# Layer 0 of a four-layer convolution network on one core: rows of x and residual rows are issued from GpSimd's queue instead of SP's

## The chip, the core and the metric

The program runs on one core of one Trainium2 chip. The metric is the device time of one execution in microseconds (us); lower is better. Three runs of the kernel before gave 6715.55, 6727.29 and 6740.69 us, with a median of 6727.29 us. Engines are named as in the profile: PE is TensorE's matmul and PEld its weight load, DVE is VectorE, ACT is ScalarE, POOL is GpSimd and SP is SyncE. A "q" behind a name (SPq, POOLq) is that engine's own sequence of waits and DMA issues.

## The reference, cut to what matters

The input x has the shape (4, 64, 256, 256) in float32. Four layers follow one another, each of the form x + f(group_norm(x)). Only layer 0 is touched by the change:

```
x = x + _L0_conv_ref(_gn(x), w_in, w_dw, fft_filter, w_out)

def _L0_conv_ref(x, w_in, w_dw, fft_filter, w_out):
    x = einsum('bchw,oc->bohw', x, w_in)            # 64 -> 384 channels
    xf = rfft2(x in 8x8 patches) * fft_filter ; x = irfft2(xf)
    x = conv2d(x, w_dw, padding=1, groups=384)      # depthwise 3x3
    x1, x2 = split(x, 2, axis=1)
    return einsum('bchw,oc->bohw', gelu(x1) * x2, w_out)   # 192 -> 64
```

Layers 1 to 3 are a 3x3 convolution, a gated "center or periphery" convolution, and a truncated Fourier layer.

## The kernel before, in words

**Tiling of layer 0.** A picture has 32 rows of 8x8 patches. One row of patches of one picture is a tile `x` of 128 partitions (64 channels times two halves of the width) by 8 lines of 128 values. `load_x` (line 414) loads it with two DMAs of 256 KB, one for each half of the width (line 418); on the side of the memory each line is a run of 128 floats, 512 bytes. `normalize_x` (L256) turns the tile into `xn` on ACT. `p_x` has four such tiles, which are shared with the tiles `st`, from which the statistics of the next picture are taken (lines 614 to 618, runs of 4 KB).

**Blocks.** The work goes in 12 blocks `p`, three for each picture, of up to 12 rows of patches. In a block, four channel groups `kb` follow one another. Each has an *expand phase* of 11 or 12 calls of `expand` (PE at line 443 multiplies `xn` with `win`; ACT and DVE copy the result to `u`, lines 450 to 452) and then 12 calls of `convolve` (g = 0 to 11; PE at lines 483 and 492; Gelu on ACT at line 499, product on DVE at line 500, result `h`). Each `h` is stored to a scratch tensor `g` in the memory by POOL (line 503); four `h` tiles take turns (`p_h`), so the Gelu of step g+4 needs the store of step g to have landed.

**The block before is projected meanwhile.** After g = 1, 4, 7 and 10, `project` does one half of one line r (0 to 7) of the block before: SP loads the needed planes of `g` (`load_g`, lines 535 and 539), `load_r` (line 548) loads the residual lines `r` of x with two DMAs of 320 or 352 KB, again in runs of 512 bytes, PE multiplies (lines 580 and 587), DVE adds into `r` (lines 596, 599, 601) and takes statistics (L607), and after the second half POOL stores `r` (line 611, two DMAs in runs of 512 bytes). Two `r` tiles take turns, so `load_r` of line r+2 must wait for the stores of line r to have landed. The weights `w` are loaded by SP (line 460). After the last block, the projection of it runs alone (the *tail*), with three `r` tiles.

**What sets the order.** A block of the program (`tc.manual_schedule`) keeps PE, DVE, ACT and SP in the order in which the program is written. POOL isn't in that list: the framework's planner sets the order of POOL's instructions, and with it the place of each DMA that POOL issues. The framework also puts in the waits: the DMAs of one kind of queue use eight semaphores in turn, so a DMA waits for the one issued eight places ahead of it, besides waiting for its tile to be free.

Of the kernel before, what the change touches and what calls it, by code (L numbers as in the profile page):

```python
# [121 lines left out]
class _Net:  # L122
# [152 lines left out]
    def _layer0(self, ctx, dst):  # L275
        tc, nc, a, B, H, W = self.tc, self.nc, self.a, self.B, self.H, self.W
# [9 lines left out]
        P = PATCH  # L286
        HW2 = W // 2
# [10 lines left out]
        halves = [slice(0, C), slice(C, 128)]  # L298
# [9 lines left out]
        p_xn, p_x = pool("l0xn", NR + 1), pool("l0x", 4)  # L308
# [20 lines left out]
        p_s = ctx_a.enter_context(tc.tile_pool(name="l0as", bufs=7))  # L329
# [73 lines left out]
        xns, x0, wl, st, gs, bst0s, bst1, loads, rts = ({} for _ in range(9))  # L403
# [7 lines left out]
            (blocks[p][0], blocks[p][1] + t) for t in range(NR + 1) if 0 <= blocks[p][1] + t < NP  # L411
        ]

        def load_x(row, p_x=p_x):
            b, i = row
            x0[row] = p_x.tile([128, P, HW2], F32, tag="x", name=f"x0_{b}_{i}")
            for s in range(2):
                nc.sync.dma_start(x0[row][halves[s]], a["x"][b, :, P * i : P * i + P, s * HW2 : (s + 1) * HW2])

        def normalize_x(row):  # L420
            b, i = row
# [94 lines left out]
        def rows_in(p, r):  # L516

            b, i0 = blocks[p]
            lo, hi = (max(0, -i0), NR) if r < P - 1 else (0, min(NR, NP - 1 - i0))
            return lo, hi, i0 + lo + (r == P - 1), (r + 1) % P  # L520
# [23 lines left out]
        def load_r(p, r):  # L544
            lo, hi, j0, rr = rows_in(p, r)
            rt = rts[p, r] = sources[p == NB - 1][2].tile([128, NR, HW2], F32, tag="r", name=f"r_{p}_{r}")[:, 0 : hi - lo]
            for s in range(2):
                nc.sync.dma_start(
                    rt[halves[s]], xr(a["x"][blocks[p][0]])[rr][:, j0 : j0 + hi - lo, s * HW2 : (s + 1) * HW2]
                )  # L550

        def load_half(p, r, half):
            if 0 <= p < NB and r < P:
                if half == 0:
                    load_r(p, r)
                load_g(p, r, half)
# [73 lines left out]
        with ordered:  # L630
# [24 lines left out]
                first_stats(k + 7)  # L655
            rows = rows_of(0)
            for row in rows[:7]:
                load_x(row, p_s)
            for row in rows[7:11]:
                load_x(row)  # L660
            for j in range(3):
                load_w(j)
            self.group_norm(0, 0, bst0, avgs)
# [18 lines left out]
            for p in range(NB + 1):  # L682
# [22 lines left out]
                b, i0 = blocks[p]  # L705
# [8 lines left out]
                for kb in range(4):  # L714
                    for t in range(NR + 1):
                        if 0 <= i0 + t < NP:
                            expand(p, kb, t)
                    for g in range(NG):
                        G = NG * kb + g
                        if g % 2 == 0:  # L720
                            load_w(p * (HID // 8) + G // 2 + 3)
                        convolve(p, kb, g)
                        if g < NG - 1:
                            self.next_norms()
                        if g in (1, 4, 7, 10):
                            unit()
                        if kb < 3:
                            if g % 3 == 0:
                                if len(loaded) == 2 or not nk:
                                    for k in loaded[: 1 if nk else 2]:  # L730
                                        next_stats(b + 1, loaded.pop(0))
                                if nk:
                                    k = nk.pop(0)
                                    load_stats(b + 1, k)
                                    loaded.append(k)
                            if kb == 2 and g == NG - 1:
                                for row in fresh[:4]:
                                    load_x(row)
                        elif 0 <= g - 1 < len(fresh):
                            k = g - 1  # L740
                            normalize_x(fresh[k])
                            if k + 4 < len(fresh):
                                load_x(fresh[k + 4])
# [731 lines left out]
```

## Time and profile before

| what | value |
|---|---|
| median of 3 runs (lowest, highest) | 6727.29 us (6715.55, 6740.69) |
| the profiled execution's own time | 6742.27 us |
| its span, first to last instruction | 6740.5 us |
| layer 0 | about 0 to 4165 us of the span |
| of it: tables, statistics, first rows | about 0 to 118 us |
| of it: tail (last block's projection alone) | about 4040 to 4163 us |
| PE busy in 340 to 4030 us | 3263.54 of 3690 us |
| DMA engines busy in 340 to 4030 us | 0.75 of 16 engines, 208 GB/s |
| POOL busy in 340 to 4030 us | 536.62 us |

The time of layer 0 follows from the page's lines of it: the first and the last store of `r` (line 611) start at 452.8 and 4165.5 us. In the page, part 3 gives the DMA queues. q1 is the queue that SP issues to, q10 the one of ACT, q0 the one of POOL, and q8 brings the engines their instructions. "Packets" are the units in which a queue's DMAs are worked off, and the share is the time that they took of the 16 DMA engines' span. In lists of waits, `PE psu L443 <- issue` means that PE stood idle ahead of a matmul of line 443 and that no other engine's work was what it waited for. The times of matmuls are modelled[...].

### The profile page before, as it was taken

What the parts mean: (1) busy time and instruction counts of PE and PEld (TensorE: products, weight loads), DVE (VectorE), ACT (ScalarE), POOL (GpSimd) and SP (SyncE); (2) the same over time, 40 slices, a digit from 0 to 9 for tenths busy, and PEclk for the clock granted to TensorE, in tenths of its full rate; (3) what the DMA queues carried; (4) which work ended last, traced back from release to release, by engine and by line L of the source; (5) the groups of instructions that cost most, each with busy time, mean ns of one, the idle gap of its engine ahead of it and who ended that gap; (6) DMA issues with size and microseconds to landing.
All of it is one profiled execution on the core that took longest, in us unless ns stands there. A gap on an engine that the chain in (4) does not pass through costs nothing.

```text
span 6740.5 us, 255130 instructions
## 1 busy us (share of the span) xinstructions
PE 5980.4 (89%) x115416; PEld 3144.4 (47%) x115416; DVE 4125.0 (61%) x5652; ACT 3098.0 (46%) x4292; POOL 1050.2 (16%) x1646
## 2 busy tenths in 40 slices
PE   3988888888888888888999885999899999999988
PEld 1445444445444545444455443333344444443476
DVE  5545454555454555454554454999788888885355
ACT  4343433343333343334333331777787777774211
POOL 3111111111111111111111110111022222221011
PEclk9999999999999999999999996999999999999855
DMA  8577778777777777777777759999766666667889
GB/s 238 154 192 207 213 210 216 206 213 207 212 210 216 207 213 207 215 210 208 206 208 206 204 175 239 241 228 228 178 169 172 177 168 177 168 176 251 322 348 400
DMA packets 878574, 1448.75 MB, mean 215 GB/s; under 512 B 77252, under 2 KB 586452, under 8 KB 875444
## 3 DMA queue, kind: packets, MB, share of 16 engines
q1 hardware_dynamic: 725284, 923.09, 54.0%
q0 software_dynamic: 148672, 500.14, 21.2%
q8 instruction: 911, 14.93, 1.0%
q10 hardware_dynamic: 3536, 9.20, 0.6%
q14 instruction: 171, 1.40, 0.1%
HBM read 932.08 MB, written 500.04 MB: 212 GB/s over the span
## 4 chain that ended last, share of the span: by engine, by line
PE 78%; issue 7%; DMA 6%; ACT 4%; DVE 4%; SPq 0%; POOL 0%; ACTq 0%; DVEq 0%; POOLq 0%
PE pc L492 17%; PE pc L483 12%; PE psu L443 11%; PE m L858 10%; PE one L1099 8%; PE div L1058 6%; PE po L580 4%; DMA x<-x 2%; PE po L587 2%; PE psz L1088 2%; DMA g<-g 2%; PE psa L1286 2%; PE psy L1433 1%; ACT u L450 1%; ACT u L452 1%
## 5 line engine op out<-in xcount | busy, mean ns | idle before, releaser
L443 PE MATMUL psu<-win,xn 64*64 64x96 f32 x34816 | 1003.8, 266 | 399.8 <-issue 323.9
L500 DVE TENSOR_TENSOR h<-h,pc 128x374 f32<-128x374 f32 x1152 | 574.7, 541 | 1269.6 <-ACT h L499 1268.5
L499 ACT ACTIVATE h<-pc 128x374 f32<-128x374 f32 x1152 | 492.8, 480 | 1827.8 <-PE pc L492 1815.9
L492 PE MATMUL pc<-u,w 64*16 64x374 f32 (+2 forms) x27648 | 1247.8, 484 | 0.2 <-issue 0.2
L443 PEld LDWEIGHTS psu<-win,xn 64*64 64x64 f32 x34816 | 908.0, 148 | 516.5 <-issue 384.1
L483 PE MATMUL pc<-u,w 64*64 64x374 f32 x9216 | 912.6, 493 | 70.6 <-DVE u L452 69.1
L503 POOL DMA_DIRECT2D g<-h x576 | 416.7, 723 | 3211.9 <-DVE h L500 2998.7
L492 PEld LDWEIGHTS pc<-u,w 64*16 64x16 f32 (+2 forms) x27648 | 414.6, 92 | 769.6 <-issue 767.9
L1044 DVE TENSOR_TENSOR q<-xn 128x2313 f32<-128x2313 f32 (+2 forms) x256 | 627.9, 2495 | 1.9 <-ACT xn L256 1.7
L1099 PE MATMUL one<-z,wp 32*32 32x512 f32 x16384 | 599.0, 598 | 19.8 <-issue 16.4
L450 DVE COPY u<-psu 128x384 f32<-128x384 f32 x544 | 303.7, 558 | 490.2 <-PE psu L443 462.9
L256 ACT ACTIVATE xn<-x,nb,r 128x1024 f32<-128x1024 f32 (+3 forms) x272 | 486.8, 1793 | 242.6 <-DMA x<-x 142.0
L483 PEld LDWEIGHTS pc<-u,w 64*64 64x64 f32 x9216 | 340.0, 133 | 516.6 <-issue 353.6
L1045 ACT ACTIVATE q<-q 128x2313 f32<-128x2313 f32 (+2 forms) x256 | 529.0, 2086 | 29.6 <-DVE q L1044 28.7
L450 ACT COPY u<-psu 128x384 f32<-128x384 f32 x544 | 288.3, 530 | 530.2 <-PE psu L443 522.9
L1058 PE MATMUL div<-q,ones 64*32 64x512 f32 x8192 | 471.2, 600 | 14.6 <-ACT q L1045 9.4
L1099 PEld LDWEIGHTS one<-z,wp 32*32 32x32 f32 x16384 | 367.1, 103 | 233.6 <-issue 93.1
L1132 POOL DMA_DIRECT2D x<-r x512 | 275.4, 547 | 977.8 <-DVE r L1129 953.7
L580 PE MATMUL po<-g,wo 128*64 128x176 f32 (+1 forms) x3072 | 315.0, 348 | 62.1 <-DMA g<-g 39.2
L858 PE MATMUL m<-t,wk 64*64 64x512 f32 x3072 | 341.1, 588 | 0.0
L580 PEld LDWEIGHTS po<-g,wo 128*64 128x64 f32 x3072 | 210.3, 141 | 212.9 <-issue 114.9
L452 DVE COPY u<-psu 64x384 f32<-64x384 f32 x544 | 304.9, 560 | 7.4
(158 smaller groups left out, 6440.0 us busy)
## 6 DMA issues: line engine op xcount, KB each, us to landing
g<-h POOLq DMA_DIRECT2D x576, 374.0 KB, 7.1
x<-x SPq DMA_DIRECT2D x240, 640.0 KB, 6.5
w<-wt SPq DMA_DIRECT2D x288, 448.0 KB, 7.9
x<-x SPq DMA_DIRECT2D x100, 1024.0 KB, 14.1
g<-g SPq DMA_DIRECT2D x414, 187.0 KB, 5.5
g<-g SPq DMA_DIRECT2D x736, 93.5 KB, 6.1
x<-in_x_dram SPq DMA_DIRECT2D x256, 256.0 KB, 8.2
x<-o POOLq DMA_DIRECT2D x128, 512.0 KB, 8.2
```

What stands on the lines that cost most here:

```text
L443: nc.tensor.matmul(ps[s][halves[1 - odd], k, at], xn[halves[s], n + odd].rearrange("p r w -> p (r w)"), win[halves[s], kb, PB * (1 - odd) ...
L450: copy(at(slice(0, 128), 8 * s + 1), v[:, 0:PB])
L483: nc.tensor.matmul(out(C * c, C, k, h), w[halves[h], k, 2 * (G % 2) + c, 0:C], cells(h, 4 * g + 2 * k + c, 0, 0), start=True, stop=False, ...
L492: nc.tensor.matmul(out(q, m, k, h), w[halves[h], k, 2 * (G % 2) + c, c0 : c0 + m], cells(h, 4 * g + 2 * k + c, down, right), start=False, ...
L499: nc.scalar.activation(h[:, k], ps[k][:, 0, 0:L], AF.Gelu)
L500: nc.vector.tensor_mul(h[:, k], h[:, k], ps[k][:, 1, 0:L])
L580: nc.tensor.matmul(out(k, s, x), wo1, moving(g1[:, 2 * k], 2 * half + k, s, x), start=(x == 0), stop=False, skip_group_check=True,)
L858: nc.tensor.matmul(rows2(m)[halves[j], s], w[dx][halves[s]], ts[n][halves[s], i, 2 * j : 2 * j + 2, dx : dx + W], start=(dx == 0), stop=(d ...
L1044: nc.vector.tensor_sub(d, p0, p1)
L1045: nc.scalar.activation(d, d, AF.Square)
L1058: ins = nc.tensor.matmul(ps[quarters[j], h], ones[halves[h]], q[n, g, k][halves[h], r + 2 * j : r + 2 * j + 2, o : o + W], start=(m == 0), ...
L1099: ins = nc.tensor.matmul(rows2(ps[g])[quarters[j], k], w[quarters[i]], z[quarters[i], h, 2 * j + dy : 2 * j + dy + 2, dx : dx + W], tile_p ...
```

## The change

`load_x` gets an argument `queue`, which is POOL's by default, and `load_r` issues from POOL. The first 11 rows of the program (22 DMAs) still come from SP. So 117 of 128 rows of x (234 DMAs of 256 KB) and all 96 residual tiles (192 DMAs of 320 or 352 KB), 426 DMAs, are issued by POOL. What is transferred, and in which runs, stays the same.

```
-        def load_x(row, p_x=p_x):
+        def load_x(row, p_x=p_x, queue=nc.gpsimd):
...
             for s in range(2):
-                nc.sync.dma_start(x0[row][halves[s]], a["x"][b, :, P * i : P * i + P, s * HW2 : (s + 1) * HW2])
+                queue.dma_start(x0[row][halves[s]], a["x"][b, :, P * i : P * i + P, s * HW2 : (s + 1) * HW2])
...
             for s in range(2):
-                nc.sync.dma_start(
+                nc.gpsimd.dma_start(
                     rt[halves[s]], xr(a["x"][blocks[p][0]])[rr][:, j0 : j0 + hi - lo, s * HW2 : (s + 1) * HW2]
                 )
...
             for row in rows[:7]:
-                load_x(row, p_s)
+                load_x(row, p_s, nc.sync)
             for row in rows[7:11]:
-                load_x(row)
+                load_x(row, queue=nc.sync)
```

On PE, DVE and ACT the order of the instructions is the same in both programs. On SP the 426 DMAs are gone from between the loads of `g`, `w` and `st`. On POOL the planner put them between the stores. Here is the compiled order of POOL's queue in block 1 (counted from 0), channel group 3, around g = 4 (the number behind h is g, and what stands in brackets is what the DMA waits for besides the semaphore of the DMA eight places ahead):

```
L503 store h 4
L418 load x, fresh row 7, first half   [ACT: its tile was normalized]
L611 store r line 6, both halves       [DVE: line 6 was added]
L418 load x, fresh row 7, second half
L548 load r line 0 of block 1, first half   [the two stores of r line 6, just above, have landed]
L503 store h 5                         [DVE]
L418 load x, fresh row 8, both halves  [ACT]
L548 load r line 0, second half
L503 store h 6                         [DVE]
L418 load x, fresh row 9, both halves  [ACT]
L503 store h 7                         [DVE]
```

In channel groups 0 to 2 the same stands there without the rows of x: store h 4, store r (both halves), load r (first half, waits for the two stores), store h 5, load r (second half), store h 6. The same pair of r store and r load stands between h 10 and h 11. The first four rows of x of a block are placed in channel group 2, between the stores of h 5 and h 10.

## The prediction

> **What bounds the kernel now.** I read the page's parts 1 to 3, then what PE waited for in the steady part of layer 0 (340 to 4030 us), then the windows, queues and order of time of single stretches.
>
> ```profile
> PE 5980.4 (89%) x115416; PEld 3144.4 (47%) x115416; DVE 4125.0 (61%) x5652; ACT 3098.0 (46%) x4292; POOL 1050.2 (16%) x1646
> ...
> q1 hardware_dynamic: 725284, 923.09, 54.0%
> q0 software_dynamic: 148672, 500.14, 21.2%
> q8 instruction: 911, 14.93, 1.0%
> ```
>
> PE is the bound; POOL has room. A packet on q0 is 3.4 KB (500.14 MB / 148672) although the residual stores in it are runs of 512 bytes, so this queue joins runs. One on q1 is 1.3 KB. q8 brings instructions in pieces of 16 KB.
>
> ```profile
> PE psu L443 <- issue: 312.7, 177, 5.9
> PE pc L483 <- DVE u L452: 65.2, 53, 2.5
> PE psu L443 <- ACT u L452: 37.7, 112, 1.2
> ```
>
> In layer 0's steady part PE waits for no data load at all. Its largest wait, 312.7 us, is "issue", and nearly all of it is in the expand phases. There are 44 full ones there, so 7.1 us in each. The next view (window, PE, PEld, DVE, ACT, POOL, clock, DMA share, GB/s) says when:
>
> ```profile
> 3802.00:3814.00 12.00, 8.80 (x296) 7.98 (x292) 6.95 (x14) 6.41 (x13) 1.06 (x2) 0.86 0.92 267
> 3815.00:3827.00 12.00, 9.60 (x383) 8.63 (x380) 9.31 (x17) 8.69 (x17) 0.00 (x0) 1.00 0.02 4
> 655.00:667.00 12.00, 8.64 (x272) 7.98 (x270) 6.83 (x13) 6.30 (x13) 0.00 (x0) 0.78 1.04 201
> ```
>
> The first two rows are halves of one expand phase. With the DMA engines busy PE gets through 296 matmuls in 12 us, with them idle 383. The third row has the DMA engines full of rows of x and residual rows: 272 matmuls, and only 201 GB/s. Its queue:
>
> ```profile
> q1 hardware_dynamic: 4111, 2.37, 102.1%
> ```
>
> That is 1.021 x 16 x 12 us / 4111 = 48 ns for each packet of about 512 bytes. So the runs of 512 bytes fill the DMA engines at a poor rate, and while these are full PE's instructions come late.
>
> In the tail (4040 to 4160 us) the DMA engines are the bound outright:
>
> ```profile
> q1 hardware_dynamic: 15073, 15.17, 57.2%
> q10 hardware_dynamic: 3536, 9.20, 31.2%
> q0 software_dynamic: 1789, 5.76, 14.7%
> ```
>
> Here a q0 packet of 3.2 KB, nearly all from stores in runs of 512 bytes, takes 0.147 x 16 x 120 / 1789 = 158 ns. That is 25 ns for 512 bytes, against 48.
>
> **What the Trainium skill says.** (1) "DMA: Bandwidth & Descriptors", section "SWDGE vs HWDGE vs iDMA": GpSimd's DMAs have their descriptors made by software, and a packet preferably holds up to 4096 bytes. The 3.4 KB agree for stores; no load on q0 is in this trace. (2) Same page, "Issuing engines are not separate DMA queues": all queues share the 16 engines, and another issuer saves only issue time. If that were all, nothing would be won here; the 48 against 25 ns speak against "only". (3) "Runtime: NRT & Kernel Launch", "Instruction fetch mechanics": instructions come in blocks of 16 KiB through a DMA queue of the engine's own, "mostly hidden". q8's piece agrees, the 312.7 us say that here it isn't hidden. (4) First page, "Anatomy of one DMA": a semaphore wait is held by the issuing sequencer. So a wait for a tile now holds up POOL's stores; no trace here shows it yet.
>
> **Part by part.** The sum is made against the profiled execution's own 6742.3 us (span 6740.5), 15.0 us above the median of the runs.
>
> *Rows of x.* Summed for each expand phase in order of time, the "issue" waits average 9.0 us in channel group 0 and 8.4 in group 3, 5.7 and 5.6 in groups 1 and 2. Rows of x are loaded just there: in group 3's expand phase, and in its steps up to group 0's. The excess is 3.0 us in 22 phases, 67 us. After, the first four rows are issued some 10 us earlier, and a row of 4 KB per partition should be one packet instead of eight. I take two thirds, **-45 us**; ends 0 and -67.
>
> *Residual rows.* Half of the 88 pairs fall to the expand phases, one each: 2 x 704 packets x 48 ns / 16 = 4.2 us of full DMA engines, after at 25 ns 2.2 us. An expand phase loses 7.1 us in some 20 us of busy DMA engines, 0.35 us for each; 2.0 x 0.35 x 44 = 31 us. I take **-26**, since residual loads now start nearer to the phase's start; ends 0 and -31.
>
> *Tail.* 16 residual DMAs of about 700 runs, 11,200 x (48 - 25) ns / 16 = 16 us of a stretch that is full of DMA. The loads of `g` also wait for one another there; **-12**; ends 0 and -16.
>
> *SP relieved.* SP held these issues up to 9.3 us, and its loads of `g` and `w` come sooner. PE waits for neither outside the tail, so 0.
>
> *POOL's own time.* A load isn't in the POOL trace; the nearest row is the residual store, 0.78 us for 640 to 704 runs. 426 x 0.78 = 332 us on an engine that is busy 537 of 3690. Cost 0, save two issues ahead of the first block's clearing of `u`, **+1.5**. Its cover is POOL's idle time between stores, 2.8 us of each 3.5; where that is gone, see next.
>
> *The new wait.* A residual load stands behind the stores it waits for, and the store of `h` 5 behind the load. In block 2, channel group 2 (POOL, then ACT):
>
> ```profile
> 948.87 1.58 POOL L611 DMA_DIRECT2D x<-r  x2 [1.70 <-DVE r L601]
> 952.16 0.75 POOL L503 DMA_DIRECT2D g<-h  x1 [1.71 <-DVE h L500]
> ```
> ```profile
> 966.71 0.86 ACT L499 ACTIVATE h<-pc 128x374 f32<-128x374 f32 x2 [2.68 <-PE pc L492]
> ```
>
> The second store starts at 949.66. Landing takes 7.4 us (median), then 0.75 for the load, then 7.1 for the store of h 5: 949.66 + 15.25 = 964.9. The Gelu of step 9, which needs that tile, starts at 966.71, and PE bears 2.0 more (a step of 3.52 us less 1.51 from Gelu to product). With 1.5 us for the residual load ahead in the same queue: 966.4. It fits by 2.3 us, so **0** in groups 0 to 2; ends 0 and the rival's. After h 11 an expand phase follows and hides all. In group 3, rows of x are queued too. From the second store (702.2) the limit is 18.3 us away (Gelu 9 at 718.45 undelayed, plus 2.0). I need 7.4 + 1 (rows of x ahead) + 0.75 + 7.1 + 1.5 = 17.8; h 6 follows two more rows and a load, and comes some 1 us late. **+17** (11 x 1.5); a gain is excluded.
>
> *Rows of x delayed behind it.* ACT waits for x for 58 us already, 1.7 us a time, and PE none of it; 0, and part of the 17 if late.
>
> Sum: -45 - 26 - 12 + 1.5 + 17 = -64.5; 6742.3 - 64.5 = 6677.8, against the median **6663 us**.
>
> **The rivals.**
>
> *POOL's queue becomes the bound (slower).* The place is channel step 9, the price what the two landings exceed: it decides once they come to more than about 17 us together (19.05 to the limit, less 0.75 and 1.5), 14.5 now. The largest landings in the trace are 10.1 and 10.3. At 9 us each: 20.25 against 19.05, 1.2 us x 33 = 40; in group 3 (3.0 + 2.5) x 11 = 60. With such landings half of the gain on x and residual rows stays (-36) and none in the tail: 40 + 60 + 1.5 - 36 = +66, **6793**. For it: q0 takes the stores and the loads in one line. Against: the DMA engines are meant to be emptier.
>
> *Nothing is joined (no change).* Loads on q0 take 48 ns for 512 bytes as before. Only the better spread of x is left, some -12, against +1.5 and +17: +7, **6734**. For it: only stores are seen on q0.
>
> *Instruction waits nearly vanish.* With the DMA engines idle, an expand phase of block 0 still loses 0.6 to 3.0 us, so about 2 x 44 stay of 312: -224, and -16 in the tail: **6487**. Against: `g`, `w` and `st` still load in these phases.
>
> **How the numbers follow.** As computed 0.48, POOL as the bound 0.24, nothing joined 0.21, waits vanish 0.07. The range 6575 to 6800 holds the first three up to the far ends of the unknowns (-114 with everything, and a little more) and leaves out the last and the worse half of the second. About 0.5%, 34 us, is what a measurement tells from no change: faster 0.55, same 0.21, slower 0.24.
>
> **What would show it.** Right: q0's packets stay above 3 KB with the rows of x in it, the DMA share between 340 and 4030 us falls from 0.75 to 0.66 or so (some 225,000 runs x 23 ns / 16 = 324 of 3690 us), "issue" ahead of L443 falls below 250 us and most in groups 0 and 3, the tail is shorter by 10 us. Wrong: ACT's Gelu (L499) waits for the landing of `g<-h`, POOL waits 7 us behind each pair of L611 and PE waits at L483; or q0 packets near 512 bytes.

## The result, and the profile after

Seven runs of the changed kernel gave a median of 6752.49 us (6744.85 to 6768.93), seven of the kernel before on the same chip 6723.85 us (6708.15 to 6740.69). The ratio is 1.0047, with a 95% interval of 1.003 to 1.0064: the change costs some 29 us where a gain of 64 was forecast. The profiled execution of the changed kernel took 6752.49 us, its span is 6750.7.

The page of the changed kernel, its busy engines and its DMA queues (packets, MB, share):

```profile
PE 5975.4 (89%) x115416; PEld 3131.8 (46%) x115416; DVE 4123.0 (61%) x5652; ACT 3098.8 (46%) x4292; POOL 1360.0 (20%) x2072
...
q1 hardware_dynamic: 467588, 794.62, 44.1%
q0 software_dynamic: 187872, 628.61, 29.5%
q8 instruction: 911, 14.93, 1.0%
```

q0 took over 128.47 MB in 39,200 packets, 3.28 KB each: the runs of 512 bytes are joined, as forecast. Yet they are not as cheap as forecast. q1's share fell by 9.9 points of 16 x 6740 us, which is 41 ns for each of the 257,696 packets gone. q0's rose by some 9,000 us of engine time, 230 ns for each new packet, or 36 ns for 512 bytes if the stores in the same queue kept their price; the forecast had 48 and 25. The same sums over the other runs that move x or r give 41 to 50 ns on q1 and 33 to 38 on q0. The DMA engines' share between 340 and 4030 us (the column before the last; before: 0.75) shows it:

```profile
340.00:4030.00 3690.00, 3240.24 (x71955) 1795.48 (x71945) 1886.85 (x3306) 1366.91 (x2697) 820.06 (x1114) 0.96 0.72 206
```

What PE waited for in the same stretch of the changed kernel (us, times, longest):

```profile
PE psu L443 <- issue: 238.5, 167, 5.1
PE pc L483 <- DVE u L452: 65.7, 54, 2.5
PE pc L483 <- DVE h L500: 53.0, 18, 5.7
PE psu L443 <- ACT u L452: 36.8, 107, 2.4
```

"issue" fell by 74 us, from 312.7. The third line is new: a convolution waits for a bank of PSUM (the memory that PE writes its results to), because DVE's product is late, because Gelu is late. With the projection's and the expand phase's waits for the same product (16.8 and 14.0 us) PE lost 84 us so. Why Gelu is late, and what stands behind that, is in the waits of ACT and of POOL; neither line exists in the kernel before:

```profile
ACT h L499 <- DMA g<-h: 187.9, 43, 8.1
```
```profile
POOL r L548 <- DMA x<-r: 514.1, 64, 12.5
```

Gelu waits 43 times until the store of an `h` has landed and frees its tile. POOL stands 64 times, 8.0 us each, ahead of a load of residual rows, until the store that it issued just before has landed. The place in block 2 that the prediction worked out (channel group 2), now with the change; POOL first, then ACT:

```profile
946.18 1.60 POOL L611 DMA_DIRECT2D x<-r  x2 [1.69 <-DVE r L601]
954.61 0.79 POOL L548 DMA_DIRECT2D r<-in_x_dram  x1 [6.83 <-DMA x<-r]
955.39 0.75 POOL L503 DMA_DIRECT2D g<-h  x1
956.13 0.82 POOL L548 DMA_DIRECT2D r<-in_x_dram  x1
957.00 1.37 POOL L418 DMA_DIRECT2D x<-in_x_dram  x2
958.36 0.75 POOL L503 DMA_DIRECT2D g<-h  x1
```
```profile
964.07 0.86 ACT L499 ACTIVATE h<-pc 128x374 f32<-128x374 f32 x2 [2.68 <-PE pc L492]
972.22 0.85 ACT L499 ACTIVATE h<-pc 128x374 f32<-128x374 f32 x2 [7.29 <-DMA g<-h]
```

The bracket of L548 is the wait for the residual stores; behind it stood the stores of h 5 and h 6. The Gelu at 964.07 just gets the tile of h 5. That of h 6 was stored at 958.36, behind two residual loads and a row of x in q0, and landed 13.8 us later. In channel group 3 the same block shows more:

```profile
1032.47 1.60 POOL L611 DMA_DIRECT2D x<-r  x2 [0.98 <-DVE r L601]
1035.94 0.70 POOL L418 DMA_DIRECT2D x<-in_x_dram  x1 [1.87 <-DMA x<-in_x_dram]
1047.24 0.79 POOL L548 DMA_DIRECT2D r<-in_x_dram  x1 [10.60 <-DMA x<-r]
1048.02 0.75 POOL L503 DMA_DIRECT2D g<-h  x1
```

The residual load here is line 0 of the next projection, which is needed only in the next block. It holds POOL for 10.6 us, and with it h 5, h 6 and the rows of x behind them.

In the tail a q0 packet holds 3.2 KB as before, but takes 0.395 x 16 x 110 / 3442 = 202 ns against 158, now that loads are among them. The queues in 4070 to 4180 us:

```profile
q0 software_dynamic: 3442, 11.13, 39.5%
q1 hardware_dynamic: 3527, 9.03, 31.7%
q10 hardware_dynamic: 3504, 9.00, 30.2%
```

From the trace in order of time comes the mean length of the phases in blocks 1 to 11, in us. An expand phase runs from its first copy on ACT to the first Gelu, a convolution from there to the next expand phase. The rows from r_only on come from the experiments. The ratios are to the kernel before in the same comparison, since it took 6724 us in the first and 6700 to 6702 in the later ones.

| kernel | expand, groups 0 / 1 / 2 / 3 | convolution, groups 0 / 1 / 2 / 3 | ratio (95%) |
|---|---|---|---|
| before | 35.8 / 31.2 / 31.5 / 34.9 | 49.6 / 49.2 / 49.0 / 50.2 | 1 |
| changed | 31.7 / 31.8 / 31.1 / 31.0 | 49.3 / 49.3 / 52.2 / 57.9 | 1.0047 (1.003-1.0064) |
| r_only | 31.3 / 30.9 / 30.9 / 34.6 | 49.2 / 49.3 / 49.3 / 55.0 | 1.0008 (0.9995-1.0022) |
| x_only | 34.7 / 31.7 / 30.5 / 33.5 | 49.4 / 49.0 / 49.5 / 50.6 | 0.9975 (0.9966-0.9985) |
| h5 | 31.4 / 31.3 / 31.1 / 33.0 | 49.4 / 49.1 / 49.4 / 55.6 | 1.0006 (0.9996-1.0015) |
| x_only_h5 | 32.7 / 31.8 / 31.1 / 32.5 | 49.3 / 49.3 / 49.7 / 50.7 | 0.9976 (0.9966-0.9987) |
| early | 34.7 / 31.3 / 31.2 / 33.4 | 49.3 / 49.1 / 49.0 / 49.9 | 1.0007 (0.9996-1.0018) |
| r_first | 32.6 / 31.3 / 30.7 / 32.9 | 49.7 / 49.1 / 49.9 / 57.2 | 1.005 (1.0038-1.0063) |
| r_first_behind | 34.8 / 31.7 / 31.0 / 32.4 | 49.5 / 49.3 / 50.1 / 51.1 | 0.9973 (0.996-0.9986) |
| r_paced | 31.1 / 31.3 / 30.2 / 31.2 | 49.6 / 50.0 / 50.4 / 60.7 | 1.0066 (1.0053-1.0079) |
| r_paced_h5 | 31.1 / 30.6 / 29.7 / 30.8 | 49.4 / 49.6 / 50.7 / 59.6 | 1.003 (1.0019-1.0041) |
| r_behind | 31.7 / 30.2 / 30.3 / 31.4 | 50.2 / 49.7 / 50.1 / 52.8 | 0.9928 (0.9906-0.9949) |
| r_behind_h5 | 31.3 / 30.7 / 29.9 / 31.4 | 50.1 / 49.9 / 50.1 / 52.9 | 0.9935 (0.9915-0.9954) |
| r_only_behind | 31.0 / 30.6 / 30.3 / 32.8 | 50.3 / 50.0 / 49.6 / 53.8 | 0.9972 (0.9961-0.9984) |

For the changed kernel the rows give -86 us in the expand phases (11 of each), +34 in group 2's convolution (3.14 x 11) and +77 in group 3's (7.75 x 10), -2 in groups 0 and 1. With -8 in the tail that is +15; block 1 starts 3.4 us later too, and layer 0's last pair of stores of `r` starts 19.2 us later (4183.95 against 4164.75).

Two limits of this table. A mean of eleven expand phases has a standard error of 0.4 to 0.9 us, so a difference of 1 us there says little. And each row is one execution, and the one of the kernel before took long: 6742 us, 18 over the median of its comparison. Differences to its row therefore flatter every other kernel, by some 5 to 40 us in all: the rows put `early` some 37 us under the kernel before, where its ratio is 1.0007.

The waits are not the whole of the +77. In group 3's convolutions PE waits 5.3 us for DVE's product, and the granted clock is 0.963 in the mean where it was 1.000; 3.7% of 57.9 us is some 2.1 us more (an estimate). Block 5's is an example: the window before, then after (PEclk is the third number from the end), and PE around the wait:

```profile
2031.03:2082.43 51.40, 51.21 (x938) 23.16 (x939) 23.28 (x44) 22.77 (x36) 14.02 (x18) 1.00 0.95 258
2011.83:2073.02 61.19, 54.04 (x918) 23.66 (x922) 22.12 (x42) 23.00 (x36) 24.52 (x33) 0.94 0.91 245
```
```profile
2053.36 2.14 PE L492 MATMUL pc<-u,w 64*16 64x374 f32 x48
2065.68 1.53 PE L483 MATMUL pc<-u,w 64*64 64x374 f32 x8 [5.67 <-DVE h L500]
2067.14 3.96 PE L492 MATMUL pc<-u,w 64*16 64x374 f32 x48
```

The same 48 matmuls take 3.96 us after the wait instead of 2.14. The trace grants half the clock there for 6.8 us.

### The profile page after: what moved, and what is told of

Read it like the earlier page. It is cut to its first block, busy times and chain, and to the rows that moved or that the text cites. A ratio compares the mean times of both kernels' runs of the same rounds, so it can differ in the third digit from the quotient of the medians.

```text
span 6750.7 us, 254994 instructions
## 1 busy us (share of the span) xinstructions
PE 5975.4 (89%) x115416; PEld 3131.8 (46%) x115416; DVE 4123.0 (61%) x5652; ACT 3098.8 (46%) x4292; POOL 1360.0 (20%) x2072
## 4 chain that ended last, share of the span: by engine, by line
PE 69%; DMA 13%; issue 8%; DVE 4%; ACT 4%; POOL 2%; SPq 0%; POOLq 0%; ACTq 0%; DVEq 0%
PE pc L492 13%; PE m L858 10%; PE psu L443 9%; PE pc L483 9%; PE one L1099 8%; PE div L1058 6%; DMA g<-h 3%; DMA x<-r 3%; PE po L580 3%; PE psz L1088 2%; DMA x<-in_x_dram 2%; DMA g<-g 2%; PE psa L1286 2%; DMA x<-x 2%; PE po L587 2%
## 5 line engine op out<-in xcount | busy, mean ns | idle before, releaser
L443 PE MATMUL psu<-win,xn 64*64 64x96 f32 x34816 | 988.6, 262 | 346.1 <-issue 247.9
L443 PEld LDWEIGHTS psu<-win,xn 64*64 64x64 f32 x34816 | 890.3, 145 | 467.9 <-issue 312.6
L483 PE MATMUL pc<-u,w 64*64 64x374 f32 x9216 | 915.4, 492 | 127.6 <-DVE u L452 69.6
L1099 PE MATMUL one<-z,wp 32*32 32x512 f32 x16384 | 596.0, 598 | 20.2 <-issue 16.0
L483 PEld LDWEIGHTS pc<-u,w 64*64 64x64 f32 x9216 | 338.7, 133 | 577.0 <-issue 345.7
L1045 ACT ACTIVATE q<-q 128x2313 f32<-128x2313 f32 (+2 forms) x256 | 529.0, 2087 | 32.2 <-DVE q L1044 31.1
L580 PE MATMUL po<-g,wo 128*64 128x176 f32 (+1 forms) x3072 | 315.4, 348 | 62.9 <-DMA g<-g 43.2
```

The lines of the kernel that those rows point to most:

```text
L443: nc.tensor.matmul(ps[s][halves[1 - odd], k, at], xn[halves[s], n + odd].rearrange("p r w -> p (r w)"), win[halves[s], kb, PB * (1 - odd) ...
L483: nc.tensor.matmul(out(C * c, C, k, h), w[halves[h], k, 2 * (G % 2) + c, 0:C], cells(h, 4 * g + 2 * k + c, 0, 0), start=True, stop=False, ...
L580: nc.tensor.matmul(out(k, s, x), wo1, moving(g1[:, 2 * k], 2 * half + k, s, x), start=(x == 0), stop=False, skip_group_check=True,)
L1045: nc.scalar.activation(d, d, AF.Square)
L1099: ins = nc.tensor.matmul(rows2(ps[g])[quarters[j], k], w[quarters[i]], z[quarters[i], h, 2 * j + dy : 2 * j + dy + 2, dx : dx + W], tile_p ...
```

## The experiments

The theory after the result (W in the later runs): POOL stands in front of a residual load, and what is late are the stores of `h` behind it (A, with the loads of x in the same line as an accomplice; B, the wait alone). The rivals: the loads ahead of a store in the line are enough without any wait (A'), or the lost time is transfer rate (C).

**One half of the change each.** `r_only` gives `load_x` SP's queue again, `x_only` gives `load_r` SP's queue again:

```
-        def load_x(row, p_x=p_x, queue=nc.gpsimd):
+        def load_x(row, p_x=p_x, queue=nc.sync):
```
```
-                nc.gpsimd.dma_start(
+                nc.sync.dma_start(
                     rt[halves[s]], xr(a["x"][blocks[p][0]])[rr][:, j0 : j0 + hi - lo, s * HW2 : (s + 1) * HW2]
```

> Residual rows from GpSimd's queue, rows of x from SP's as in the kernel before. Theory A (the stores of h stand in GpSimd's line behind the loads of x and r, and the wait of r's load for the store just issued holds all of GpSimd, so Gelu waits for its buffer): with x gone from that line the store of the residual rows lands in about the 7 us of the kernel before, so the wait is short and no Gelu waits; only the small gains of r (-4) and of the tail (-8) are left: 6712 us, within 6700 to 6725, and under 20 us of Gelu waiting for a landing of h. Theory B (the blocking wait of r alone holds the stores, whatever else is in the line): Gelu still waits in channel groups 2 and 3, some 60 to 110 us: 6770 to 6820. Theory C (what is lost is transfer rate, not waiting): 6720 to 6730, no Gelu waits.

> Rows of x from GpSimd's queue, residual rows from SP's as in the kernel before. Theory A: the line in front of the stores of h keeps the x loads but loses the r loads and GpSimd's wait for r; the expand phases keep their -70 us, the Gelu waits shrink from 188 us to perhaps 60 to 100, of which some 30 to 60 reach TensorE: 6685 to 6715. Theory B (the blocking wait of r alone): the Gelu waits vanish and the -70 stand: 6650 to 6660. Theory A' (the x loads ahead in the line are enough): nearly all Gelu waits stay: 6740 to 6755.

Measured: `r_only` 6711.37 us and `x_only` 6684.86, against 6702.28. In `r_only` POOL still waits for the residual stores, 331.5 us in 43 waits of 7.7 us, and Gelu 62.9 us. That is B's figure for the waits and A's for the time. In `x_only` the waits are gone:

```profile
ACT xn L256 <- DMA x<-in_x_dram: 23.0, 22, 2.0
ACT h L499 <- DMA g<-h: 2.3, 5, 0.9
```

So the rows of x ahead of the stores do no harm by themselves: A' falls. What the loss needs is the residual loads on POOL; whether it is their wait or their bytes in the line, these two runs do not tell. And `x_only` gains 17 us, where B had forecast 6650 to 6660 us: the waits went as B says, the time did not. Its expand phases save only 34 us (11 x (1.08 - 0.47 + 1.01 + 1.46)). In `r_only` they save 63 us, 50 of it in group 0, and its convolution of group 3 loses 49. Both savings are measured from the row of the kernel before, with the limits given above.

**A fifth `h` tile.** Room for it comes from keeping one buffer of the input's statistics instead of two:

```
-        p_w, p_h = pool("l0w", 4), pool("l0h", 4)
+        p_w, p_h, p_b = pool("l0w", 4), pool("l0h", 5), pool("l0b", 1)
...
-        new_bst0 = lambda b: self.sp.tile(
+        new_bst0 = lambda b: p_b.tile(
```

> The changed kernel with five h buffers instead of four (room made by keeping one buffer of the input's statistics in layer 0 instead of two). No transfer and no queue is changed; a Gelu may now run one step (7.3 us) further ahead of the landing. Theory A and theory B: all Gelu waits seen were 16.9/3 to 5.7 us in the mean, so nearly all vanish, and the 112 us that the convolution stretches of groups 2 and 3 lost come back: 6640 to 6660. Rival (the lost time is not in these waits but in the engines being fed slower): 6740 to 6755.

> Rows of x from GpSimd's queue, residual rows from SP's, five h buffers. Theory A and B: no Gelu waits, and the -70 us of the expand phases stand without the gain of r in the tail: 6650 to 6665, some 5 to 12 us over the run with five buffers and both loads moved. If the gain in the expand phases needs r off SP's queue too: 6690 to 6725.

`h5` took 6708.2 us, ratio 1.0006: some 27 us of the loss came back, not 100. Neither the theories' range nor the rival's (6740 to 6755) holds it. The Gelu waits did go, but another took their place (`h5`, ACT):

```profile
ACT xn L256 <- DMA x<-in_x_dram: 115.3, 32, 6.1
ACT h L499 <- DMA g<-h: 4.3, 1, 4.3
```

In the changed kernel the first line was 51.5 us. The loads of x stand behind the same residual load on POOL, ACT normalizes x in between the Gelus, and PE waits for ACT again: 103 of the 115 us lie in steps 9 and 10 of group 3, where the lost time is. So the wait has two followers, and a buffer for one of them uncovers the other. `x_only_h5` took 6686.82 us, the same as `x_only` within the intervals, since without POOL's wait there is nothing to cover; its expected 40 to 50 us of gain failed for the reason that `x_only`'s did. It lies just under the range given for the case that the expand phases need the residual rows off SP's queue too.

**The residual loads placed later on POOL.** A load of residual rows gets one more dependency, on DVE's product of the step in which the program issues it. The planner then puts it behind that step's store of `h`, three steps after the stores that it waits for. In `r_paced` this is done from line 2 on, in `r_paced_h5` with five `h` tiles too:

```
-                nc.vector.tensor_mul(h[:, k], h[:, k], ps[k][:, 1, 0:L])
+                self.mul = nc.vector.tensor_mul(h[:, k], h[:, k], ps[k][:, 1, 0:L])
...
-                nc.gpsimd.dma_start(
+                load = nc.gpsimd.dma_start(
...
+                if r > 1:
+                    self.after(load, self.mul)
```

`r_first` moves x and only line 0 of the residual rows to POOL, without that dependency. `early` is the kernel before with the first four rows of x two steps earlier:

```
-                nc.gpsimd.dma_start(
+                (nc.sync if r else nc.gpsimd).dma_start(
```
```
-                            if kb == 2 and g == NG - 1:
+                            if kb == 2 and g == 9:
```

> The changed kernel, with each load of residual rows (from the third on) given one more dependency, on VectorE's product of the convolution step in which the program issues it. GpSimd's order then has the load three steps behind the store that frees its buffer, where GpSimd finds it landed, instead of right behind it. Bytes, queues, packets and buffers are those of the changed kernel. Theory W (the loss is GpSimd standing for 8 us in front of a load of residual rows, and with it the stores of h and the loads of x behind it): GpSimd's 514 us of waiting for the residual store and the Gelu waits of 188 us go, the convolution stretches of groups 2 and 3 come back to about 49.3 and 50.5 us, and the expand phases keep most of their gain (group 0 about 31.5, group 3 about 33.5 us): some 60 us under the kernel before, ratio 0.988 to 0.993. Rival L (the bytes of the residual rows in GpSimd's line, 0.66 MB more per pair of groups, delay the stores whoever waits): Gelu waits of 60 us or more stay, ratio 0.998 to 1.004.

> The same as the run with the later residual loads, with five h buffers too. Theory W: there is no Gelu wait left for a fifth buffer to cover: the same time as with four, within 5 us, ratio 0.988 to 0.993. Rival L: the fifth buffer takes another 20 us or more.

> Rows of x from GpSimd's queue; of the residual rows only the first load of each block (which is issued at the block's start and waits for no store just issued) from GpSimd's, the other seven from SP's. It tells where the gain of channel group 0's expand phase comes from (35.8 us before, 34.7 with x alone moved, 31.3 with the residual rows alone moved). If the 512-byte packets of the block's first residual load, issued from SP just ahead of that expand phase, are the cause: group 0 falls to about 31.5 us, with no wait in GpSimd and no Gelu wait: 17 + 35 = about 50 us under the kernel before, ratio 0.991 to 0.994. If it comes from the later residual loads: as with x alone moved, ratio 0.997 to 0.999.

> The kernel before, everything from SP's queue, with the first four rows of x for the next block loaded two convolution steps earlier (step 9 of channel group 2 instead of step 11). In the changed kernel GpSimd, whose order is not written by hand, issues these rows several steps earlier than SP did. If group 3's expand phase (34.9 us before, 31.0 after) is slow because those loads run beside it, and not because of their packets' size: the phase falls to about 32 us without any joined packet, -30 us, ratio 0.995 to 0.997. If the size of the packets is what costs: 34 to 35 us and ratio 0.999 to 1.001.

`r_paced` took 6741.56 us (ratio 1.0066), `r_first` 6730.93 (1.005): both far off what theory W said, and `r_paced` above rival L's range as well. Where the time is lost said why. In `r_paced` group 2 came back from 52.2 to 50.4 us, but group 3 went to 60.7; in `r_first` group 3's convolution alone is long. `r_first` has but ten of the waits, one in each of ten blocks, in steps 7 and 8 of group 3. Here are the residual stores, the load of line 0 for the next block, and the two Gelus that follow on it (`r_first`, block 2, POOL, then ACT):

```profile
1025.39 1.63 POOL L611 DMA_DIRECT2D x<-r  x2 [0.99 <-DVE r L601]
1027.36 0.70 POOL L418 DMA_DIRECT2D x<-in_x_dram  x1 [0.35 <-DMA x<-in_x_dram]
1039.86 0.79 POOL L548 DMA_DIRECT2D r<-in_x_dram  x1 [11.80 <-DMA x<-r]
1040.64 0.75 POOL L503 DMA_DIRECT2D g<-h  x1
```
```profile
1046.63 0.85 ACT L499 ACTIVATE h<-pc 128x374 f32<-128x374 f32 x2 [4.31 <-DMA g<-h]
1053.98 0.85 ACT L499 ACTIVATE h<-pc 128x374 f32<-128x374 f32 x2 [3.65 <-DMA g<-h]
```

Written at the start of the next block, this load had been put by the planner right behind the store that frees its tile. I had exempted lines 0 and 1 in `r_paced`, and so left the costliest wait where it was; why group 3 takes longer still than in the changed kernel (57.9) was not settled. `r_paced_h5` (6718.59 us, 1.003) repeats what `h5` showed: no Gelu waits, 148 us of waiting for x. Its 23 us under `r_paced` meet rival L's mark of 20, and so do not speak against L. `early` took 6705.82 us, no difference. Its expand phase of group 3 reads 33.4 us instead of 34.9, but group 0's, which the edit doesn't touch, reads 1.1 us less too, so no effect of the loads' moment is shown.

**All residual loads placed later.** `r_behind` is `r_paced` without the `if r > 1`; `r_behind_h5` has five `h` tiles too; `r_only_behind` leaves the rows of x on SP; `r_first_behind` is `r_first` with the dependency on line 0 alone.

> As the run with the later residual loads, but for all of them, the first two of each block too: each load of residual rows depends on VectorE's product of the convolution step in which (or just ahead of which) the program issues it. In the two runs before, 7 to 10 waits of 11 to 12 us in GpSimd were left in steps 7 and 8 of channel group 3: the next block's first residual load, which GpSimd's order had right behind the store that frees its buffer, among the loads of x. Theory W (those waits, and nothing else, made group 3's convolution 57 to 61 us long): group 3's convolution falls to about 50.5 us, no Gelu waits, expand phases 31.3 / 31.3 / 30.5 / 33 us: about 65 us under the kernel before, ratio 0.989 to 0.994. Rival L (the residual rows' bytes in GpSimd's line): group 3 stays above 55 us, ratio 1.000 to 1.006.

> Rows of x and each block's first residual load from GpSimd's queue, that load behind the last store of h of the block before; the other seven residual loads from SP's. The run without this placing was 34 us over the kernel before. Theory W: ten waits of 11.4 us were the whole of its loss: group 3's convolution 57.2 to about 50.6 us, ratio 0.993 to 0.9965. Rival L: no change, ratio 1.003 to 1.006.

> Only the residual rows from GpSimd's queue, rows of x from SP's, each residual load placed as in the run with all of them later. Theory W: without that placing the two sides cancelled (group 0's expand phase -50 us, group 3's convolution +50 us); with it the +50 go: ratio 0.991 to 0.9945. Rival L: ratio 0.999 to 1.002.

> All residual loads placed later, and five h buffers. Theory W: nothing left to cover, the same as with four buffers within 5 us, ratio 0.989 to 0.994. Rival L: 10 us or more under the run with four buffers.

The same place in `r_first_behind` (the inserted lines make the store of `r` L613):

```profile
1030.28 0.80 POOL L613 DMA_DIRECT2D x<-r  x1 [0.74 <-DVE r L603]
1031.40 0.78 POOL L613 DMA_DIRECT2D x<-r  x1 [0.32 <-DMA x<-in_x_dram]
1032.43 0.70 POOL L418 DMA_DIRECT2D x<-in_x_dram  x1 [0.25 <-DMA x<-in_x_dram]
1034.36 0.75 POOL L503 DMA_DIRECT2D g<-h  x1 [1.24 <-DMA g<-h]
...
1060.40 1.59 POOL L548 DMA_DIRECT2D r<-in_x_dram  x2 [0.47 <-issue]
```
```profile
1048.12 0.86 ACT L499 ACTIVATE h<-pc 128x374 f32<-128x374 f32 x2 [1.55 <-PE pc L492]
1051.64 0.85 ACT L499 ACTIVATE h<-pc 128x374 f32<-128x374 f32 x2 [0.54 <-PE pc L492]
```

The store of h 5 is issued 2.2 us after the residual stores instead of 13.6, and the Gelus wait for PE again. Group 3's convolution falls from 57.2 to 51.1 us, the ratio from 1.005 to 0.9973, just outside theory W's range (0.993 to 0.9965): ten waits of POOL, 113.6 us by its list, cost the program some 52 us (0.0077 x 6700; 35 to 69 at the ends of the two intervals). By the rows group 3's convolution gives 61 us and group 0's expand phase takes 24 back (32.6 to 34.8), since line 0 is now loaded within it. `r_behind` took 6654.98 us against 6701.61, ratio 0.9928 (0.9906 to 0.9949), 34 to 63 us less than the kernel before, with the same bytes, queues and packets as the changed kernel. POOL's waits for residual stores fall from 514.1 to 11.1 us; ACT's waits are:

```profile
ACT xn L256 <- DMA x<-in_x_dram: 70.2, 38, 3.4
ACT h L499 <- DMA g<-h: 7.1, 16, 0.8
```

Theory W stands: the residual loads still stand ahead of stores of `h` in the line, and group 3 is under rival L's 55 us. Of the 80 us between the changed kernel and this one (0.0119 x 6700), the rows put 59 in the convolutions and 21 in the expand phases, of which those of groups 1 and 2 are shorter (they carry less traffic now that the loads stand elsewhere). `r_behind_h5` (6661.62 us) shows nothing more to cover. `r_only_behind` (6686.2 us, 0.9972) was expected at 0.991 to 0.9945 and is off: its convolution of group 3 is still 53.8 us. Its ACT waits 136.4 us for rows of x, which come from SP there. Why these land later than in `r_behind` was not settled. Nor is it settled why group 3 stays 2.6 us over the kernel before in `r_behind`, and 2.3 over what was expected.

## Why the prediction was wrong, step by step

**Rows of x (-45) and residual rows (-26): the sum held by luck, the parts did not.** In the changed kernel the expand phases got 86 us shorter (some 68, if the extra 18 us of the row before lie there), and the waits called "issue" 74; forecast were 71. But the halves alone give 34 for x and 63 for the residual rows. I took group 0's excess for the rows of x. By these runs it comes mainly from the residual rows, whose first lines are loaded just there. In `r_first_behind`, where x and line 0 come from POOL, group 0 still takes 34.8 us, and another line is loaded from SP within it (DMA issues of block 5's phase, the last column is us to landing):

```profile
r<-in_x_dram POOLq DMA_DIRECT2D x2, 352.0 KB, 6.6
r<-in_x_dram SPq DMA_DIRECT2D x2, 352.0 KB, 7.6
```

With all residual rows moved and x not (`r_only_behind`) it takes 31.0. That the time hangs on the number of small packets, as the prediction had it, is less clear. Here are the means over the phases, each taken from 2 us before its start; in group 1 neither rows of x nor a block's first residual lines are loaded:

| expand phase | before | x_only | r_first_behind | r_only_behind | r_behind | changed |
|---|---|---|---|---|---|---|
| group 0: packets under 2 KB | 3383 | 2860 | 2078 | 902 | 703 | 671 |
| MB | 6.28 | 6.15 | 6.25 | 5.77 | 5.69 | 5.32 |
| us | 35.8 | 34.7 | 34.8 | 31.0 | 31.7 | 31.7 |
| group 1: packets under 2 KB | 2014 | 1987 | 2002 | 698 | 661 | 630 |
| MB | 4.25 | 4.21 | 4.23 | 3.86 | 3.74 | 4.24 |
| us | 31.2 | 31.7 | 31.7 | 30.6 | 30.2 | 31.8 |
| group 3: packets under 2 KB | 5715 | 2282 | 2244 | 4355 | 902 | 654 |
| MB | 5.33 | 4.80 | 4.63 | 4.88 | 4.53 | 4.57 |
| us | 34.9 | 33.5 | 32.4 | 32.8 | 31.4 | 31.0 |

In groups 0 and 3 the phases with few small packets are the short ones. But they also have fewer bytes, by up to 15%, and the DMA engines are busy for less time in them (group 0: 24.6 us before, 20.2 changed). In group 1 the changed kernel has 1384 fewer small packets than the kernel before at the same bytes, and the phase is no shorter. `x_only_h5`, with 2900 small packets and 6.26 MB in group 0, took 32.7 us there where `x_only` took 34.7. In group 3 the moment changed with the packets: before, all eight DMAs of the next block's first four rows are issued in the phase or up to 2 us ahead of it, in the changed kernel none (the planner put all of them 4.7 us or more ahead). So small packets alone do not set the time; packets, bytes, moment and the engines' busy time were not separated.

What "issue" is, the traces do settle. In the kernel before all 143 such waits of 0.5 us or more ahead of L443 end 1.2 to 1.8 us after a packet of q8, the queue of instructions, is through; in the changed kernel all 128 do. The waits of L483 for DVE's copy end anywhere from 0.2 to 4.9 us after one. So PE waited for its instructions. Not separated from that is the clock: over group 0's expand phases it was granted at 0.869 before and 0.913 after, in group 3's at 0.864 and 0.935. The three windows that the prediction compares have 0.86, 1.00 and 0.78, so their counts of matmuls don't show the DMA engines' part alone.

**Tail (-12): -8.** From the last Gelu to the last store it took 127 us before, 118 in `r_only` and 130 in `x_only`, which fits the mechanism; the size was off, since a joined load costs 36 ns for 512 bytes, not 25.

**DMA share (0.66 forecast): 0.72.** The 25 ns were those of stores, taken for loads too, and the 48 those of a stretch in which the DMA engines were full; 41 and 36 were measured.

**POOL's own time (0) and SP relieved (0): held.** No load of `g` or `w` shows among PE's waits in the steady part. The 9.3 us that SP held an issue were one of the first rows, which SP still loads; of the loads moved none was held for more than 3.85 us. POOL is busy 820 of 3690 us between 340 and 4030 us, 283 more for about 390 more DMAs, 0.73 us each.

**The new wait (0 in groups 0 to 2, +17 in group 3): the step that failed.** Measured +34 in group 2 and +77 in group 3, and nothing in groups 0 and 1. The forecast laid the place out rightly, step 9 and a limit of 18.3 us, and then filled it with landings from a queue that held stores only. By its own sum (17.8 against 18.3) h 5 was in time in group 3 too, and the 17 us stood for h 6 alone. In group 3 of block 2 the second residual store, with rows of x ahead of it, landed after 13.3 us where the forecast gave 8.4 (7.4 + 1); in `r_first` POOL's wait alone was 10.6 to 12.3 us. In group 2 the stores landed as forecast and h 5 was in time, but the forecast followed only h 5: h 6, behind two residual loads and a row of x, landed after 13.8 us, and its Gelu waited 7.3. The forecast also had no term for the clock after such waits, some 2 of the 7.75 us of a block's group 3.

**Rows of x delayed behind it (0):** the same wait delays them; the Gelu waits hid this in the changed kernel, and `h5` brought it out (+64 us of ACT's waiting).

**The rival that came true** is POOL's queue as the bound, with its place and its mark of 17 us for two landings. Its time of 6793 was 40 us too high: groups 0 and 1 lost nothing, and the gain on the expand phases, of which it kept half, was kept.

Of the signs named for "wrong", the three of the wait came: Gelu waiting for `g<-h`, POOL waiting 8.0 us in the mean behind 64 pairs of L611, PE waiting at L483. Of those named for "right", the packets above 3 KB and the 238.5 us of "issue" came too: the gains were there, and the wait outweighed them. What the Trainium skill says in "DMA: Bandwidth & Descriptors", section "Anatomy of one DMA", that the issuing sequencer holds the wait, is now shown: 11.80 us, with everything behind it. Its section "Issuing engines are not separate DMA queues", that another issuer saves issue time only, does not hold here: GpSimd's queue made packets of 3.28 KB of the same runs of 512 bytes, at 36 ns for 512 against 41 (by the sums over the queues).

## What to carry to other kernels

Before a load goes to another engine's queue, list in the compiled order what it waits for there and what stands behind it. If its tile is freed by a store of the same queue, it should stand a landing's length behind that store, and the landing is to be taken with the new loads in the queue, not from the old trace. If a wait has two followers, a buffer for one only uncovers the other; moving the waiting instruction (here 0.9928 instead of 1.0047) helps both.

## What the runs showed of the hardware

GpSimd's queue joined runs of 512 bytes from the memory into packets of 3.28 KB. For the same bytes the packets took 36 ns per 512 instead of 41 in the changed kernel, and 33 to 38 instead of 41 to 50 over the runs; the stores' 25 ns were not reached. A DMA that GpSimd issues waits on GpSimd: 11.80 us in front of one load, with the stores behind it. In a queue with rows of x ahead, a residual store landed after 13.3 us, where the median was 7.4 before. PE's waits called "issue" end 1.2 to 1.8 us after a packet of instructions is through. After a wait of 5.67 us, 48 matmuls took 3.96 us instead of 2.14, at half the granted clock.
